# Scatters of a routed token group taken out of the routing job and spread over the attention stage

## The chip, the cores and the metric

The kernel runs on one core of one Trainium2 chip. A core has a matrix engine (TensorE; PE in the profile, its weight loads PEld), a vector engine (VectorE, DVE), an activation engine (ScalarE, ACT), a general engine (GpSimd, POOL), and a queue engine that issues most transfers (SyncE, SP). Each engine takes its instructions in the order in which they stand in its own list; between engines they wait on semaphores. The metric is the device time of one launch in microseconds (us).

## The reference

Eight sequences of 1024 tokens with 256 features go through causal attention with 16 heads, a residual, and a mixture of experts (8 experts, two chosen for each token), with a residual again.

```python
x = x + _layernorm(_L0_attn_ref(_layernorm(x), Wq, Wk, Wv, Wo))     # 16 heads of 16, causal softmax
logits = flat @ router_weight.T + router_bias                        # flat = _layernorm(x)
topk_w, topk_idx = jax.lax.top_k(softmax(logits), 2)
gu   = jnp.einsum('th,ehn->ten', flat, gate_up_proj) + gate_up_bias  # E=8, H=256, 2I=1024
glu  = min(gu[..., :I], 7) * sigmoid(1.702 * min(gu[..., :I], 7))
down = jnp.einsum('tei,eih->teh', (clip(gu[..., I:], -7, 7) + 1) * glu, down_proj) + down_bias
x = x + _layernorm((gathered(down, topk_idx) * topk_w).sum(axis=1))
```

Everything is float32. The kernel computes only the two chosen experts of a token: it sorts the tokens by expert through DRAM.

## The kernel before, in words

**Attention stage.** The work is cut into 32 units: eight sequences (b) times four groups of four heads (g). A unit has nine steps, each of them two half steps (one pair of heads each), so 18 half steps. In a half step PE computes scores for the row maxima of the unit (`sa`, line 834), the transposed scores of the unit before (`sb`, line 929) and weighted values (`av`, line 970). VectorE reduces the maxima (lines 844 to 865, 888), ScalarE takes the exponentials (line 941), and GpSimd masks the diagonal blocks (lines 883 and 950). Masks exist only in five of the nine steps; the last four steps of a unit (WHOLE) have none. A 33rd pass drains the last unit.

**Background work.** All the rest of that stage (layer norms, projections, the output projection, routing) is written as generators that yield `piece(pe, dve, act, pool, after)`: an estimated cost on four engines, and for how many half steps the next piece must wait. They are jobs in three lists: `urgent`, `due`, `back`. After each half step `pump` adds to a credit per engine and emits the pieces that are ready and that the credit allows, lists in that order, jobs in the order in which they were started. A piece's instructions stand in the engines' lists at that point; a GpSimd instruction is tied to its place by `in_order` (a scatter comes after the last ordinary GpSimd instruction before it, and the next ordinary one comes after all scatters before it).

**Groups and routing.** The 8192 tokens are 16 groups (NT) of 512; group t = 2b + c. `finish(b, c)`, a job of the list `back`, projects the attention's output (`yps`, line 1031), normalises it, adds the residual, stores it, and goes on with `route(t, ...)`: layer norm into the tile `xn2` (two buffers), transposes (`x2ps`, line 1092), router logits, the ranks of the experts on VectorE (lines 1109 to 1149), counts on PE (`cps`, line 1153), a slot per token and choice (lines 1158 to 1183), two extra columns in `xn2` (lines 1185 and 1190), and then eight indirect DMAs (two choices times four row blocks, line 1194), the scatters, which write 128 rows each to their experts' regions in DRAM. After group 12 of 16 (NT - LATE) and after the last one, `route` also builds a table (lines 304 to 439): which expert and which rows each later tile takes.

**Expert stage.** Tiles of 256 rows of one expert go through the gate and up products (`gu`, line 1470), the activation, and the down product (`dn`, line 1510). The first 16 tiles (EARLY) come from the first 12 groups alone, and go by the first table; while the first 14 of them run, `pump` is called between their products, so that the last groups are routed beside them. Ahead of tile 14 of the order, `finish_all()` emits what is left of all jobs at once, as tile 16 needs the second table. Loads run two tiles ahead. The early loads (`load_early`) stand, at the latest, after the last half step of unit 31, half step 575; if the first table is not known there, pieces are emitted one after another, with nothing between them, until it is:

```python
while NT - LATE not in known:
    emit(back, back[0])
load_early()
```

Of the kernel before, what the change touches and what calls it, by code (L numbers as in the profile page):

```python
# [24 lines left out]
def piece(pe=0.0, dve=0.0, act=0.0, pool=0.0, after=0):  # L25


    return (pe, dve, act, pool), after
# [30 lines left out]
def attn_moe_kernel(  # L59
# [15 lines left out]
    nc = tc.nc  # L75
    B, S, D = x.shape
# [4 lines left out]
    NG = H // HG  # L81
# [9 lines left out]
    NT = B * S // TB  # L91
    NTB = TB // P
    I32 = mybir.dt.int32
    TOPK = 2
    TS = 256
    TN = TS // P
# [142 lines left out]
    def in_order(put, scatter=False):  # L239

        if free[0]:
            return
        for before_it in fixed if scatter else fixed + loose:
            tc.add_manual_dep(
                put.ins, before_it,
                mybir.DependencyInfo(mybir.DependencyClass.NoSync, mybir.DependencyReason.DATA),
                reason="order of the source",
            )
        if scatter:
            loose.append(put.ins.name)  # L250
        else:
            fixed[:], loose[:] = [put.ins.name], []

    def apart(put, group):

        tc.declare_no_dep(put.ins, group=group, reason="scatters to different rows")
        tc.add_to_no_dep_group(group, put.ins)
# [30 lines left out]
    LATE = 4  # L288
# [253 lines left out]
    with ExitStack() as attn:  # L542
# [514 lines left out]
        def normed(dst, src):  # L1057
# [13 lines left out]
                )  # L1071
            yield piece(after=1)

        def route(t, x1, last):

            xn = ap2.tile([P, NTB, XD], F32, tag="xn2", name=f"xn2_{t}")
            if t >= NT - TN - 1:
                yield from normed(xn, x1)
# [109 lines left out]
            first_of = ap2.tile([P, NTB, E], F32, tag="rank", name=f"first_{t}")  # L1188
            nc.vector.tensor_tensor(first_of, is_r[:, 0], region, ALU.mult)
            nc.vector.tensor_reduce(xn[:, :, D + 1], first_of, AX.X, ALU.add)  # L1190
            for r in range(TOPK):
                for n in range(NTB):
                    yield piece(pool=1.1, after=0 if last and (n or r) else 1)
                    put = nc.gpsimd.indirect_dma_start(  # L1194
                        out=xs_dram[:, :],
                        out_offset=bass.IndirectOffsetOnAxis(ap=slots[:, t, r, n : n + 1], axis=0),
                        in_=xn[:, n, :], in_offset=None,
                    )
                    in_order(put, scatter=True)
                    apart(put, "xs")  # L1200
            if nth == NT - 1:
                yield piece(dve=0.4)
                fill_tails()
# [9 lines left out]
        def start(kind, gen):  # L1213
            job = Job(gen, now)
            kind.append(job)
            return job

        def emit(kind, job):
            job.run(now)
            if job.done:  # L1220
                kind.remove(job)
# [52 lines left out]

        early = {}

        def load_early():

            flat = x_buffer("early")
            for i in range(IN_X):  # L1280
                early[i] = flat[:, ts(i, XS)].rearrange("p (n d) -> p n d", n=TN)
                at = loaded(tables[NT - LATE][:, 1, i : i + 1], E * R)
                ahead_of(nc.sync.dma_start(out=early[i], in_=slot_rows(at)), "xs")
# [3 lines left out]
        with tc.manual_schedule(  # L1287
            engines={engines.PE, engines.DVE, engines.Activation, engines.SP}
        ):
            free[0] = False  # L1290
            jobs = {}
            wr = begin()
            more = start(due, others(wr))
            for _ in range(2 * KT):
                emit(due, more)
            jobs["v"] = start(due, values(0))
            jobs["p1"] = start(due, project(0, 1))
            second, late, whole = None, deque(), False
            for u in range(B * NG + 1):
                first = None  # L1300
                if u < B * NG:
                    b, g = divmod(u, NG)
                    if g == 1:
                        finish_by(jobs["v"], jobs["p1"])
                        if b + 1 < B:
                            jobs["x"] = start(due, prep(b + 1))
                    if g < NG - 1:
                        spread(u + 1)
                    if b + 1 < B and g == 2:
                        jobs["p0"] = start(due, project(b + 1, 0))  # L1310
                    first = maxima_tiles(u)
                for k in range(K):
                    if second:

                        for c in {t[0] for t in STEPS[k][2]}:
                            while not rows_of[u - 1, c].done:
                                emit(urgent, rows_of[u - 1, c])
                    if u == B * NG - 1 and not early and NT - LATE in known:
                        load_early()
                    if first and g == 0 and b + 1 < B and k == 5:  # L1320
                        xs[b + 1] = load_x(b + 1)
                    if first and g == NG - 1 and b + 1 < B and k == K - 2:
                        finish_by(jobs["p0"])
                        spread(u + 1)
                    if first and g == NG - 1 and b + 1 < B and k == K - 4:
                        jobs["v"] = start(due, values(b + 1))
                        jobs["p1"] = start(due, project(b + 1, 1))
                    for pair in range(2):
                        if not first and pair:
                            break  # L1330
                        heads = []
                        if first:
                            heads.append(first[0](k, pair))
                            if second:
                                heads.append(second[0](k, 1 - pair))
                        else:
                            heads += [second[0](k, 0), second[0](k, 1)]
                        for part in range(2):
                            for scores, _ in heads:
                                for hh in range(2):  # L1340
                                    scores(hh, part)


                        for _, use in reversed(heads) if first else heads:
                            use()

                        us = 1.64 + 0.62
                        of_dve = {WHOLE: 1.22, EDGE: 1.68, TWO: 0.72}[STEPS[k][0]]
                        of_act = 1.8 if STEPS[k][0] == TWO else 1.2
                        share = 0.68, us - of_dve, us - of_act, us - 0.35  # L1350
                        halves = (pair,) if first else (0, 1)
                        if first and second:
                            earn(*share)


                            if pair:
                                halves = (0, 1) if whole else (1,)
                            else:
                                whole = spend(least=1.5) is not None and bool(late) and (
                                    len({t[0] for t in STEPS[late[0][1]][2]}) == 1  # L1360
                                )
                                halves = () if whole else (0,)
                        if len(late) > DELAY - 1 or (late and not second):
                            f, kk = late[0]
                            for half in halves:
                                f(kk, half)
                            if not first or pair:
                                late.popleft()
                        if not first or pair:
                            if first:  # L1370
                                first[1](k)
                            if second:
                                second[1](k)
                                late.append((second[2], k))
                        if first and second:
                            pump(most=0.0 if whole and not pair else 1.0)
                        elif first:

                            pump(0.8, 1.2, 0.8, 1.0)
                        else:  # L1380
                            pump(1.2, 2.0, 0.8, 1.4)
                second = values_tiles(u) if first else None
                if u == B * NG - 1 and not early:
                    while NT - LATE not in known:
                        emit(back, back[0])
                    load_early()
            while late:
                f, kk = late.popleft()
                for half in range(2):
                    f(kk, half)  # L1390
            free[0] = True
# [384 lines left out]
```

## Time and profile before

| | us |
|---|---|
| median of 3 runs | 2174.46 |
| the runs | 2169.46 to 2175.39 |
| the profiled execution | 2167.24 |
| its span (first to last instruction) | 2165.1 |
| PE busy | 2057.3 (95%) |
| VectorE busy | 1708.3 (79%) |
| ScalarE busy | 1062.7 (49%) |
| GpSimd busy | 1051.7 (49%) |
| the 128 scatters (line 1194) on GpSimd | 129.1, mean 1.009 each |

Line numbers are those of the kernel before. Busy time counts a matmul from its issue to a modelled end, so a busy PE is not PE at its peak; what matters is where PE stands idle, and what it waits for. The attention stage runs to about 1348 us, its drain to 1381 us, the expert stage from there to the end. The chain of work that ended last is 71% PE, 17% VectorE and 5% GpSimd.

### The profile page before, as it was taken

How to read it: one execution, taken by the hardware profiler on the slowest of the kernel's cores; microseconds unless marked ns; L12 is line 12 of the kernel's file. 1: busy time of each engine (PE TensorE's matmuls, PEld its weight loads, DVE VectorE, ACT ScalarE, POOL GpSimd, SP SyncE). 2: the span in 40 equal slices, each digit the busy share in tenths (PEclk: the TensorE clock that was granted, in tenths of full speed). 3: DMA queues.
4: the chain of work that ended last, by engine and by line, in shares of the span. 5: the costliest groups of instructions: out<-in, count | busy, mean ns of one | idle time of the engine just before them, and what ended most of it. 6: DMA issues, size and time to landing. Idle time of an engine off the chain costs nothing.

```text
span 2165.1 us, 44591 instructions
## 1 busy us (share of the span) xinstructions
PE 2057.3 (95%) x16205; PEld 1262.3 (58%) x16205; DVE 1708.3 (79%) x4091; ACT 1062.7 (49%) x2072; POOL 1051.7 (49%) x1213
## 2 busy tenths in 40 slices
PE   7999999999999999999999998999999999999995
PEld 3444444444544434434534443678888888888884
DVE  4786886986887887887888788678778888877776
ACT  3566665666666655656655665433123232222222
POOL 3421653472474455354544645456544444444443
PEclk9999999999999999999999999999999999999998
DMA  4101102112112111112111111656867777876784
GB/s 123 23 16 44 35 26 63 32 46 46 42 32 69 24 41 46 48 36 58 46 39 41 44 39 36 207 189 208 259 242 266 269 246 262 291 241 231 268 286 150
DMA packets 147096, 254.85 MB, mean 118 GB/s; under 512 B 21504, under 2 KB 106008, under 8 KB 144952
## 3 DMA queue, kind: packets, MB, share of 16 engines
q1 hardware_dynamic: 133128, 217.01, 32.5%
q0 software_dynamic: 12528, 34.36, 4.3%
q8 instruction: 129, 2.11, 0.4%
q14 instruction: 95, 0.78, 0.1%
q10 hardware_dynamic: 1216, 0.58, 0.1%
HBM read 171.13 MB, written 55.63 MB: 105 GB/s over the span
## 4 chain that ended last, share of the span: by engine, by line
PE 71%; DVE 17%; POOL 5%; issue 3%; DMA 2%; ACT 2%; SPq 0%; DVEq 0%; ACTq 0%; POOLq 0%
PE sa L834 18%; PE gu L1470 15%; PE av L970 10%; PE dn L1510 8%; PE sb L929 6%; PE pjk L740 3%; PE yps L1031 3%; PE pjq L740 3%; PE vps L726 3%; DVE mx L850 2%; DVE sa L844 2%; DVE gate L1479 1%; PE xtps L1448 1%; DVE mx L888 1%; DVE acc L1586 1%
## 5 line engine op out<-in xcount | busy, mean ns | idle before, releaser
L941 ACT ACTIVATE pT<-sb 128x512 f32<-128x512 f32 x1134 | 616.2, 595 | 394.2 <-PE sb L929 360.6
L929 PE MATMUL sb<-qP,kP 32*128 32x512 f32 (+3 forms) x3072 | 703.6, 528 | 13.8 <-ACT pT L941 11.0
L834 PE MATMUL sa<-kP,qP 32*128 32x512 f32 (+3 forms) x3072 | 655.2, 526 | 25.5 <-DVE mx L844 12.6
L1470 PE MATMUL gu<-xsT,wg 128*128 128x256 f32 (+1 forms) x2208 | 487.5, 373 | 3.3 <-ACT xsT L1450 1.9
L1470 PEld LDWEIGHTS gu<-xsT,wg 128*128 128x128 f32 x2208 | 407.6, 191 | 59.3 <-ACT xsT L1450 4.3
L850 DVE TENSOR_REDUCE mx<-sa 128x2 f32<-128x1024 f32 x256 | 310.6, 1215 | 116.7 <-PE sb L929 96.6
L950 POOL TENSOR_SCALAR_AFFINE_SELECT pT<-pT 128x512 f32<-128x512 f32 x256 | 164.6, 659 | 468.2 <-ACT pT L941 456.1
L834 PEld LDWEIGHTS sa<-kP,qP 32*128 32x128 f32 x3072 | 226.8, 185 | 248.1 <-issue 100.0
L1481 ACT ACTIVATE sig<-gate 128x256 f32<-128x256 f32 (+1 forms) x276 | 112.8, 409 | 522.2 <-DVE gate L1479 492.0
L970 PE MATMUL av<-pT,vpad 128*32 128x256 f32 (+1 forms) x5120 | 350.0, 370 | 5.0 <-DVE avs L981 3.0
L1486 POOL TENSOR_TENSOR sig<-sig,gate 128x256 f32<-128x256 f32 (+1 forms) x276 | 195.4, 715 | 321.4 <-ACT sig L1481 317.4
L929 PEld LDWEIGHTS sb<-qP,kP 32*128 32x128 f32 x3072 | 294.9, 186 | 46.2 <-ACT pT L941 20.5
L970 PEld LDWEIGHTS av<-pT,vpad 128*32 128x32 f32 x5120 | 117.1, 109 | 292.7 <-issue 233.9
L1510 PE MATMUL dn<-wd,act 128*128 128x256 f32 x1064 | 257.7, 382 | 14.0 <-DVE act L1491 11.5
L1510 PEld LDWEIGHTS dn<-wd,act 128*128 128x128 f32 x1064 | 194.6, 190 | 45.6 <-DVE act L1491 19.4
L844 DVE CUSTOM_DVE_ANT_0 sa<-sa,cmask 128x512 f32<-128x512 f32 x256 | 177.7, 699 | 40.2 <-PE sb L929 20.8
L1479 DVE TENSOR_SCALAR gate<-gu,bs 128x256 f32<-128x256 f32 (+1 forms) x276 | 128.8, 467 | 86.2 <-PE gu L1470 70.7
L1491 DVE SCALAR_TENSOR_TENSOR act<-up,sig 128x256 f32<-128x256 f32 (+1 forms) x276 | 131.9, 478 | 49.3 <-POOL sig L1486 45.5
L1194 POOL DMA_INDIRECT xsd<-xn,slots x128 | 129.1, 1009 | 64.2 <-DVE xn L1190 34.8
L1524 POOL DMA_INDIRECT ytd<-ys,places x133 | 134.9, 1014 | 48.8 <-issue 26.9
L869 ACT COPY edge<-sa 128x512 f32<-128x512 f32 x192 | 113.0, 589 | 41.1 <-DVE mx L859 19.9
L888 DVE TENSOR_REDUCE mx<-edge 128x8 f32<-128x1024 f32 x96 | 115.7, 1205 | 17.9 <-POOL edge L883 17.9
(243 smaller groups left out, 2327.4 us busy)
## 6 DMA issues: line engine op xcount, KB each, us to landing
wg<-_L_ffn_gate_up_proj_dram SPq DMA_DIRECT2D x69, 1024.0 KB
wd<-in_L_ffn_down_proj_dram SPq DMA_DIRECT2D x69, 512.0 KB
xs<-xsd SPq DMA_DIRECT2D x60, 258.0 KB
yy<-ytd SPq DMA_DIRECT2D x15, 1024.0 KB
bs<-biasd SPq DMA_DIRECT2D x69, 132.0 KB
x<-in_L_attn_x_dram SPq DMA_DIRECT2D x16, 512.0 KB
aT<-avn SPq DMA_DIRECT2D x256, 32.0 KB
x1d<-y SPq DMA_DIRECT2D x16, 512.0 KB
```

What stands on the lines that cost most here:

```text
L834: nc.tensor.matmul(ps[:, hh, ds(at, w)], lhsT=qP[r, ts(i, P)], rhs=kP[r, ds(c * QC, w)], start=True, stop=True,)
L844: nc.vector.tensor_tensor_reduce(out=ps[:, hh, :], in0=ps[:, hh, :], in1=cmask, scale=1.0, scalar=NEG, op0=ALU.add, op1=ALU.max, accum_out ...
L850: nc.vector.tensor_reduce(mx[:, heads, i, 2:3], ps, AX.X, ALU.max)
L888: nc.vector.tensor_reduce(mx[:, :, of_two(k)[0], 1], d, AX.X, ALU.max)
L929: nc.tensor.matmul(banks[hh][:, ds(at, QC - off)], lhsT=kP[r, ts(j, P)], rhs=qP[r, ds(c * QC + off, QC - off)], start=True, stop=True,)
L941: nc.scalar.activation(pT[:, 2 * pair + hh, :], banks[hh], AF.Exp)
L950: in_order(nc.gpsimd.affine_select(out=d, in_=d, compare_op=ALU.is_ge, fill=0.0, base=0, pattern=[[0, HG], [1, P]], channel_multiplier=-1,))
L970: nc.tensor.matmul(av[ds(hh * HS, HS), ds(off + a - at, z - a)], lhsT=vp[:, j, ds((g * HG + hh) * VS, HS)], rhs=pT[:, hh, a:z],  start=c n ...
L1470: nc.tensor.matmul(ps[:, half, :w], lhsT=wg[:, kt, ds(half * FF + f * P, P)], rhs=xT[:, kt, :], start=(kt == 0), stop=(kt == KT - 1),)
L1479: nc.vector.tensor_scalar(gt, ps[:, 0, :w], bs[:, f : f + 1], LIMIT, ALU.add, ALU.min)
L1486: in_order(nc.gpsimd.tensor_tensor(sg, sg, gt, ALU.mult))
L1510: nc.tensor.matmul(pss[n][:, 0, :], lhsT=act[:, f, ts(n, P)], rhs=wd[:, f, :], start=(f == 0), stop=(f == FT - 1),)
```

## The change

The eight scatters leave `route` and become a job of their own, `scatter_rows`, in the list `back`. For groups 0 to 9 (`slow`: t < NT - LATE - TN = 10) a piece may follow the one before it only after four half steps, where it was one; for groups 10 to 14 it is one half step as before; the last group still does its own, in a row. `route(t)` now begins by waiting until group t - 2 has put all its scatters (its `xn2` buffer is the one that group t takes over). `route` itself is done, and the table is built, without waiting for the group's scatters; so the early loads ask for both: the first table known, and all scatters of groups 0 to 11 put (`early_known`). At the forced point after half step 575, the scatters that are held back are emitted first, then the first job of `back`.

```diff
+        puts = {}
+
+        def scatter_rows(t, xn, last):
+
+            slow = t < NT - LATE - TN
+            rest = 0 if last else 4 if slow else 1
+            for r in range(TOPK):
+                for n in range(NTB):
+                    yield piece(pool=1.1, after=rest if n or r else 3 if slow else 1)
+                    put = nc.gpsimd.indirect_dma_start(
...
+                    in_order(put, scatter=True)
+                    apart(put, "xs")
+
+        def scattered(t):
+            return t in puts and (t >= NT - TN or puts[t].done)
+
         def route(t, x1, last):
 
+            while t > 1 and not scattered(t - 2):
+                yield piece(after=1)
             xn = ap2.tile([P, NTB, XD], F32, tag="xn2", name=f"xn2_{t}")
...
-            for r in range(TOPK):
-                for n in range(NTB):
-                    yield piece(pool=1.1, after=0 if last and (n or r) else 1)
-                    put = nc.gpsimd.indirect_dma_start(
...
+            puts[t] = scatter_rows(t, xn, last)
+            if last:
+                yield from puts[t]
+            else:
+                puts[t] = start(back, puts[t])
...
+        def early_known():
+            return NT - LATE in known and all(scattered(t) for t in range(NT - LATE))
...
-                    if u == B * NG - 1 and not early and NT - LATE in known:
+                    if u == B * NG - 1 and not early and early_known():
                         load_early()
...
-                    while NT - LATE not in known:
-                        emit(back, back[0])
+                    while not early_known():
+                        held = [t for t in puts if t < NT - LATE and not scattered(t)]
+                        emit(back, puts[held[0]] if held else back[0])
                     load_early()
```

More of the change, by code (lines that the diff above doesn't have):

```diff
@@ L1072, in normed @@
             yield piece(after=1)
+        puts = {}
[6 more added lines that the diff above has]
+                    put = nc.gpsimd.indirect_dma_start(
+                        out=xs_dram[:, :],
+                        out_offset=bass.IndirectOffsetOnAxis(ap=slots[:, t, r, n : n + 1], axis=0),
+                        in_=xn[:, n, :], in_offset=None,
+                    )
+                    in_order(put, scatter=True)
+                    apart(put, "xs")
+        def scattered(t):
+            return t in puts and (t >= NT - TN or puts[t].done)
         def route(t, x1, last):
+            while t > 1 and not scattered(t - 2):
+                yield piece(after=1)
             xn = ap2.tile([P, NTB, XD], F32, tag="xn2", name=f"xn2_{t}")
@@ L1190, in route @@
             nc.vector.tensor_reduce(xn[:, :, D + 1], first_of, AX.X, ALU.add)
-            for r in range(TOPK):
-                for n in range(NTB):
-                    yield piece(pool=1.1, after=0 if last and (n or r) else 1)
[L1194 to L1200, printed above, removed]
+            puts[t] = scatter_rows(t, xn, last)
[3 more added lines that the diff above has]
+                puts[t] = start(back, puts[t])
             if nth == NT - 1:
```

## The prediction

> **What bounds the kernel now.** I read the page first. PE is busy for 95% of the span and 71% of the chain that ended last is PE, so time is won or lost where PE stands still. Then I cut the attention stage at the starts of its units (96 `sa` rows of line 834 each), four units, one sequence, per stretch, and added the last two units, the forced stretch after half step 575, the drain, and the end of routing in the expert stage:
>
> ```profile
> core 0: us, PE busy (x) PEld busy (x) DVE busy (x) ACT busy (x) POOL busy (x), PEclk, DMA share, GB/s
> 582.10:746.50 164.40, 161.35 (x1574) 76.19 (x1573) 136.36 (x305) 105.19 (x197) 87.95 (x96) 1.00 0.18 45
> 746.50:921.30 174.80, 167.35 (x1582) 78.00 (x1578) 140.77 (x328) 104.67 (x198) 91.04 (x99) 0.97 0.17 44
> 921.30:1095.40 174.10, 166.13 (x1582) 78.07 (x1578) 140.80 (x326) 104.47 (x198) 91.31 (x99) 0.98 0.17 45
> 1095.40:1268.60 173.20, 165.66 (x1580) 78.06 (x1576) 139.49 (x329) 103.26 (x195) 85.22 (x96) 0.98 0.16 39
> ...
> 1347.90:1353.90 6.00, 1.68 (x12) 1.28 (x10) 3.96 (x21) 0.34 (x1) 1.94 (x3) 0.67 0.01 1
> 1353.90:1381.50 27.60, 26.43 (x302) 12.09 (x301) 13.09 (x45) 18.09 (x28) 9.43 (x12) 0.89 0.52 175
> 1530.00:1560.00 30.00, 26.70 (x125) 22.77 (x124) 25.90 (x93) 4.75 (x11) 15.76 (x21) 0.94 0.91 267
> ```
>
> The same work takes 164.4 us in one sequence and 174.8, 174.1 and 173.2 in the next three, which also lose clock (0.97, 0.98). The order of time inside these three shows six places, two each, where VectorE and ScalarE both sit for 3 to 5 us as if PE were late; all six lie in or right behind four or five scatters in a row on GpSimd, in the last half steps of a unit, where no mask stands between them. One of them, GpSimd, ScalarE and VectorE:
>
> ```profile
> 775.00 0.96 POOL L1194 DMA_INDIRECT xsd<-xn,slots  x1 [0.30 <-issue]
> 776.27 0.96 POOL L1194 DMA_INDIRECT xsd<-xn,slots  x1 [0.30 <-issue]
> 777.53 0.96 POOL L1194 DMA_INDIRECT xsd<-xn,slots  x1 [0.30 <-issue]
> 778.80 0.96 POOL L1194 DMA_INDIRECT xsd<-xn,slots  x1 [0.30 <-issue]
> ```
>
> ```profile
> 774.71 1.09 ACT L941 ACTIVATE pT<-sb 128x512 f32<-128x512 f32 x2 [0.52 <-PE sb L929]
> 779.81 1.08 ACT L941 ACTIVATE pT<-sb 128x512 f32<-128x512 f32 x2 [4.01 <-PE sb L929]
> ```
>
> ```profile
> 776.48 0.18 DVE L509 BATCH_NORM_AGGREGATE mv<-st 128x2 f32<-128x6 f32 x1
> 779.70 1.23 DVE L850 TENSOR_REDUCE mx<-sa 128x2 f32<-128x1024 f32 x1 [3.04 <-PE sb L929]
> ```
>
> Scatters stand 1.27 us apart in a row; everybody resumes at 779.8, when the last ends. Last, the chain at the forced point, where routing pieces stand with nothing between them:
>
> ```profile
> 1350.97 0.18 DVE two L414
> ...
> 1351.28 0.83 PE tabps L417 x2
> ...
> 1353.22 0.14 issue
> 1353.36 0.57 PE takenps L438 x2
> 1353.93 2.02 PE sb L929 x8
> ```
>
> PE's last `av` ends at 1347.9; until 1353.9 PE has two products of the table to do and waits for VectorE between them: a forced piece costs its full latency, 6.0 us here for four pieces.
>
> **The change, part by part.** I set the order of both programs' instructions side by side. No scatter is added or dropped; places change, three in kind.
>
> *1. Fewer scatters in a row.* In the attention stage GpSimd's list had eight runs of four or five scatters: groups 0, 2, and 4 to 9. Group 2's, at 577.7 to 582.9, cost nothing visible; group 0's cost its half step 2.2 us; groups 4 to 9 are the six stalls. After the change I find one run of five (groups 4 and 5 interleaved, unit 20), two of three, the rest one or two. Three sequences at 174.8, 174.1, 173.2 against 164.4 are 28.9 us, 4.8 a stall with its lost clock. Five of six gone: -24. Bounds: -31 (all six and group 0's), 0 (the runs are not the cause).
>
> *2. The forced stretch grows.* Eight scatters at four half steps are 32 half steps, and `route(t)` waits for group t - 2, so the groups back up. In the order, group 8's scatters end in unit 31 and group 10 has only its layer norm done at half step 575, where before only the end of the table was left. Behind the last `av` now stand, one after another: three scatters of group 9, group 10's routing from its transposes on, its eight scatters, all of group 11's routing, its eight scatters, the whole table. Nothing of units 31 and 32 stands between, on PE, VectorE or ScalarE. Its latency:
> - routing from the transposes: `x2ps` 0.59, two copies 2 x 0.586, `lpsT` 0.44, copy 0.27, `lps` 0.41, VectorE lines 1109 to 1149 4.72 (the sum of the groups' means), the exponential 0.23, `cps` 0.60, VectorE lines 1158 to 1190 3.65: 12.1; eight handovers at about 0.17 (0.14 to 0.23 in the chain): 13.4;
> - eight scatters, 7 x 1.27 + 0.96 = 9.9. They are on the path: group 11's `rstd` (line 517) stands behind them on GpSimd;
> - `rstd` 1.05 and four normalisations of 1.23: 6.0;
> - group 11's routing: 13.4;
> - the table: VectorE lines 310 to 356 2.2, `segps` 0.76, copy 0.15, `firstps` 0.38, handovers 0.5, and from line 375 to the last product the measured 4.5 (1349.45 to 1353.93): 8.5. Group 11's scatters (9.9) run beside it; the drain's first masks and the early loads queue behind them, hidden while PE starts the drain and 27.6 us lie ahead of tile 0.
>
> Together 51.2, less the 6.0 of before: +45. The clock in that stretch was 0.67; at 1/0.67 the 4.1 us of products in the two routings cost 2 more. +47. Bounds: +36 (handovers nothing, and 40% of VectorE's 17 us overlapped, as neighbours at 1350.06 to 1350.34 partly are), +58 (group 11's scatters hold up the table as runs of scatters do above, twice 4.8).
>
> [...]
>
> *3. A second forced stretch.* Groups 12 to 15 start later, and at tile 14 `finish_all()`, which before found nothing left, now emits 31 pieces: group 15's routing from line 1138 on, its eight scatters, and the second table. VectorE first clears tile 13's last quarter (lines 1479 and 1483, 0.94), then 2.52, `cps` 0.6, 3.65, tails 0.35, table lines 321 to 354 4.3, `segps` 0.76, copy 0.15, `firstps` 0.38, lines 375 to 394 1.1, lines 397 to 414 2.6, `tabps` 0.83, handovers 1.0: 19.2 without PE work between. Before, these pieces lay in 1530 to 1560, where PE idled 3.3. +16. Tile 16's loads (the zeros to 1549, weights landing at 1558.4, 25 us behind the table's start) have the stretch and tiles 14 and 15 as cover; without those the wait of 25 would show. Bounds: +9 (half overlaps work queued on PE), +24 (its scatters hold VectorE up).
>
> *4. Moved work.* PE's `yps` of groups 12 and 13 (4 x 1.92) and one routing (some 2.4) go from the attention stage to the drain and the expert tiles, groups 10 and 11 into the stretch above (4.9). All of it is 15 us of PE; but units with almost none of it took 39 to 40 us (units 1 and 30) and such with much of it 39.8 to 43 (17, 16), so perhaps a third is won, 5. The drain has 1.2 us idle and the tiles 1600 to 2000 almost none, GpSimd gets 20 us more beside the early tiles, and two more activation table loads of 1.28 stand on ScalarE (idle enough): +5. Net 0; bounds -10 to +10.
>
> **Sum.** -24 + 47 + 16 + 0 = +39 on the profiled execution: 2167.2 + 39 = 2206. Its time is 7.2 under the median of the runs; carried over, 2213. I say 2211.
>
> **The rivals.**
> - *The stalls stay* (a transfer or PE itself makes them, scatters only happen to be there). For it: group 2's run of four had none. Against: six of six long waits lie there. Part 1 becomes 0: 2235.
> - *The stretches overlap more than their rows say*, both at their low bounds, 36 + 9 - 24: 2195. For it: neighbouring instructions on VectorE overlap. Against: the 6.0 us of before is what its rows add up to.
> - *Faster*: the thinned attention stage wins what the stretches cost. It would have to bring all twelve units from 746.5 to 1268.6 (43.5 each) to units 1 to 3's 38.8: 56 us, and units 4 to 17 (40.9) some 2 us each, 28: 84 against 63, 2153. It decides from a win of 70 us. Against: in 582 to 746, without stalls, PE is busy for 161 of 164 us.
> - *The change does not space the scatters.* GpSimd runs a scatter as soon as it can, whatever the plan; only masks between them hold them apart. If pairs stall too, part 1 is about halved: 2223.
>
> **How the numbers follow.** Forecast 0.62, stalls stay 0.08, overlap 0.13, spacing halved 0.11, faster 0.06. The first, the halved one and the one with the stalls are slower; so is overlap, but for low luck. A change within 0.3% (6.5 us) is about what a measurement of this kernel cannot tell from none; it would need overlap and all the low bounds: 0.03 of the 0.13, with 0.01 from the others. Faster 0.05, same 0.04, slower 0.91. The range reaches from 2185, overlap with -31 and -4 of the moved work, to 2240, the stalls staying with a little more: 0.08 is left out below, 0.08 above.
>
> **What would show it.** Right: the three sequences from unit 18 on near 164 to 168 us at clock 0.99 or more; PE idle for some 45 to 50 us in one stretch behind `av` of half step 575, with 19 scatters inside it; a second of some 17 to 20 us ahead of tile 14. Wrong: waits of 3 to 5 us on ScalarE where no scatters stand in a row; or PE working in those stretches.

## The result, and the profile after

| | us |
|---|---|
| before, median of 6 runs, the first three among them (2161.1 to 2175.4) | 2167.57 |
| after, median of 6 runs (2195.7 to 2198.3) | 2196.76 |
| ratio | 1.0129, 95% interval 1.0113 to 1.0146 |
| profiled execution, before and after | 2167.24 and 2195.73 |
| its span, before and after | 2165.1 and 2194.0 |

The changed kernel is slower by 29 us; the forecast was 2211, in a range from 2185 to 2240. A second comparison gave a larger loss, 1.0267, and much of what follows is about that difference.

The attention stage, the two stretches and the early expert tiles of the changed kernel, in windows. The columns are the window, its length, and the busy time of PE, PEld, VectorE, ScalarE and GpSimd with instruction counts, then the granted clock, the DMA share and GB/s:

```profile
576.90:741.90 165.00, 160.46 (x1576) 76.16 (x1575) 138.60 (x303) 104.91 (x198) 95.30 (x102) 1.00 0.18 46
741.90:907.50 165.60, 160.75 (x1538) 73.70 (x1538) 137.50 (x314) 102.08 (x191) 83.59 (x93) 0.98 0.19 46
907.50:1071.90 164.40, 160.50 (x1581) 76.11 (x1581) 136.87 (x305) 103.93 (x196) 82.69 (x90) 1.00 0.17 40
1071.90:1233.30 161.40, 159.57 (x1574) 75.71 (x1570) 133.81 (x300) 104.45 (x196) 69.02 (x78) 1.00 0.16 38
1303.00:1353.20 50.20, 12.22 (x70) 7.95 (x70) 21.40 (x106) 3.79 (x10) 23.71 (x24) 0.56 0.12 44
1353.20:1386.80 33.60, 31.18 (x326) 15.89 (x325) 10.96 (x33) 21.00 (x33) 12.04 (x18) 0.95 0.44 148
1386.80:1562.70 175.90, 167.06 (x848) 141.62 (x849) 133.56 (x387) 54.82 (x113) 113.56 (x126) 0.99 0.63 209
1564.70:1585.80 21.10, 4.05 (x16) 3.83 (x17) 13.81 (x66) 1.93 (x3) 10.37 (x11) 0.59 0.48 129
```

The three sequences from unit 18 on take 165.6, 164.4 and 161.4 us, where they took 174.8, 174.1 and 173.2. In 1303.0 to 1353.2 the forced pieces stand: 50.2 us with 12 us of PE, where before there were 6.0. In 1564.7 to 1585.8 the second forced stretch stands, ahead of tile 14.

The first stretch, in the order of time, PE:

```profile
1311.59 0.61 PE L1175 MATMUL cps<-chosen,ones 128*128 128x32 f32 x2
1328.43 0.47 PE L1114 MATMUL x2ps<-ident,xn 128*128 128x128 f32 x1 [16.23 <-POOL xn L529]
...
1346.41 0.98 PE L363 MATMUL segps<-ident,new 128*128 128x1 f32 x4 [5.32 <-DVE new L356]
...
1352.72 0.57 PE L438 MATMUL takenps<-each,ones 128*128 128x8 f32 x2 [1.26 <-DVE each L435]
1353.22 2.09 PE L929 MATMUL sb<-qP,kP 32*128 32x512 f32 x8
```

and what PE waited 16.23 us for, on GpSimd:

```profile
1316.17 0.95 POOL L1083 DMA_INDIRECT xsd<-xn,slots  x1 [8.51 <-issue]
...
1325.02 0.96 POOL L1083 DMA_INDIRECT xsd<-xn,slots  x1 [0.30 <-issue]
1326.01 1.04 POOL L517 TENSOR_TENSOR rstd<-ve,nhalf_seg 128x4 f32<-128x4 f32 x1
1327.15 4.83 POOL L529 TENSOR_SCALAR xn<-y,mv,rstd 128x256 f32<-128x256 f32 x4
```

Group 11's `rstd` and its four normalisations stand behind eight scatters of group 10, and its transposes behind those. The second stretch, PE:

```profile
1570.94 0.61 PE L1175 MATMUL cps<-chosen,before 128*128 128x32 f32 x2 [6.28 <-DVE chosen L1171]
...
1579.26 0.56 PE L363 MATMUL segps<-ident,new 128*128 128x1 f32 x2 [7.29 <-DVE nf L350]
...
1585.83 2.77 PE L1491 MATMUL gu<-xsT,wg 128*128 128x256 f32 x6
```

One stall is left in the attention stage, in the one run of five scatters (unit 20). GpSimd and ScalarE:

```profile
850.35 0.98 POOL L1083 DMA_INDIRECT xsd<-xn,slots  x1 [0.16 <-issue]
...
855.43 0.96 POOL L1083 DMA_INDIRECT xsd<-xn,slots  x1 [0.30 <-issue]
```

```profile
851.40 1.08 ACT L941 ACTIVATE pT<-sb 128x512 f32<-128x512 f32 x2 [0.53 <-PE sb L929]
855.95 0.60 ACT L941 ACTIVATE pT<-sb 128x512 f32<-128x512 f32 x1 [3.46 <-PE pjk L740]
```

So in this pair of profiles, in the attention stage from unit 18 on, every run of four or more scatters has its long waits (six runs before, one after). Some runs are followed, some 7 us after their last scatter, by one more wait of 3 to 4 us with no four scatters near it (834.8 and 1008.9 before, 863.6 after). It seems to follow from the stall by way of the clock, which was at 0.50 from 831.1 to 834.5 and from 1005.2 to 1008.6 before, with PE idle for 1.99 and 1.90 us ahead of that, and from 858.5 to 865.3 after, with PE idle for only 0.23 and 0.25 us. At that clock two products of `sa` took 1.22 us, at full clock 0.70.

```profile
861.38 1.22 PE L834 MATMUL sa<-kP,qP 32*128 32x512 f32 x2
```

```profile
863.61 1.09 ACT L941 ACTIVATE pT<-sb 128x512 f32<-128x512 f32 x2 [3.39 <-PE sb L929]
```

Only one such wait of before stands by itself, 3.45 us on ScalarE at 1304.8, in unit 30; on chip 10, below, it is there too (4.72 us at 1271.5).

### The profile page after: what moved, and what is told of

Read it like the earlier page. It is cut to its first block, busy times and chain, and to the rows that moved or that the text cites. A ratio compares the mean times of both kernels' runs of the same rounds, so it can differ in the third digit from the quotient of the medians.

```text
span 2194.0 us, 44614 instructions
## 1 busy us (share of the span) xinstructions
PE 2050.0 (93%) x16205; PEld 1263.8 (58%) x16205; DVE 1714.8 (78%) x4091; ACT 1065.5 (49%) x2074; POOL 1047.7 (48%) x1213
## 5 line engine op out<-in xcount | busy, mean ns | idle before, releaser
L929 PE MATMUL sb<-qP,kP 32*128 32x512 f32 (+3 forms) x3072 | 694.2, 523 | 0.5 <-issue 0.2
L950 POOL TENSOR_SCALAR_AFFINE_SELECT pT<-pT 128x512 f32<-128x512 f32 x256 | 164.2, 657 | 510.1 <-ACT pT L941 495.9
L929 PEld LDWEIGHTS sb<-qP,kP 32*128 32x128 f32 x3072 | 292.3, 184 | 29.0 <-ACT pT L941 6.9
L888 DVE TENSOR_REDUCE mx<-edge 128x8 f32<-128x1024 f32 x96 | 115.8, 1206 | 15.8 <-POOL edge L883 15.4
```

The source lines that it names most:

```text
L929: nc.tensor.matmul(banks[hh][:, ds(at, QC - off)], lhsT=kP[r, ts(j, P)], rhs=qP[r, ds(c * QC + off, QC - off)], start=True, stop=True,)
L950: in_order(nc.gpsimd.affine_select(out=d, in_=d, compare_op=ALU.is_ge, fill=0.0, base=0, pattern=[[0, HG], [1, P]], channel_multiplier=-1,))
```

## The experiments

The theory was that scatters in a row make the stalls, and that the forced pieces cost their latency. The first four runs were to tell the two prices apart. They ran on chip 11, where the kernel before took 2134.41 us (2132.1 to 2138.2), 33 us less than in the first comparison. No chip is recorded for that one.

**A limit of two scatters in a row, in the kernel before.**

```diff
                     yield piece(pool=1.1, after=0 if last and (n or r) else 1)
+                    while not free[0] and not forced and len(loose) >= 2:
+                        yield piece(pool=1.1, after=1)
...
                 if u == B * NG - 1 and not early:
+                    forced.append(True)
                     while NT - LATE not in known:
```

> The kernel before, with one rule more: a scatter of the attention stage is put off while two scatters already stand behind the last ordinary GpSimd instruction. No run of scatters is longer than two; the scatters stay in the routing job, and the forced point after half step 575 has the same four pieces as before. Runs make the stalls (my theory): the three sequences from unit 18 on fall from 174 us to 164 to 166 at a clock of 0.99 or more, nothing else moves, and the ratio to before is 0.986 to 0.989 (-24 to -31 us, six stalls at 4.8). Runs are not the cause (the thinning of the stage by work that moves out of it was what won the time): the sequences stay near 174 us, ratio 0.998 to 1.002.

Measured: 2135.8 us, ratio 1.0008 (0.9998 to 1.0018). No gain, as the rival said, but not for the rival's reason: the sequences from unit 18 on took 165.1, 164.5 and 163.6 us, not 174. The kernel before was that fast there too.

**The limit, and groups 10 and 11 held back to the forced point.**

```diff
+            while t in (10, 11) and not forced:
+                yield piece(after=1)
             xn = ap2.tile([P, NTB, XD], F32, tag="xn2", name=f"xn2_{t}")
```

> The limit of two scatters in a row, and in addition the routing of groups 10 and 11 waits for the forced point after half step 575: 79 forced pieces there against 4 (70 in the changed kernel), and 39 pieces ahead of tile 14 against none (31 in the changed kernel). The scatters of groups 0 to 9 are as in the run with the limit alone. If the forced stretches cost what the profile of the changed kernel shows (44 and 21 us) and the work moved into them and behind them is worth about 16 to 20 us to the attention stage: 50 to 65 us over the run with the limit alone, so ratio to before 1.01 to 1.02. If the price of the changed kernel comes from the waits of its spread scatters and not from the forced pieces: no more than 10 us over the run with the limit, ratio 0.99.

Measured: 2206.7 us, ratio 1.0338 (1.0321 to 1.0355), 71 us over the limit alone. Its two stretches, in windows:

```profile
1296.90:1357.40 60.50, 14.30 (x70) 8.83 (x70) 23.44 (x115) 3.70 (x9) 25.87 (x25) 0.53 0.08 30
1574.80:1596.30 21.50, 4.99 (x34) 4.31 (x35) 14.49 (x69) 2.08 (x4) 15.11 (x16) 0.57 0.57 167
```

This kernel keeps its scatters in the routing job, so pieces late enough to be forced make the loss by themselves; spread scatters are not needed for it. By the profiles, against the limit alone: attention stage -19, first stretch +55, drain +6, early tiles +8, second stretch +23, sum +71 as measured. The stage won as much as expected (16 to 20); the expectation of 50 to 65 was short by a first stretch of 60.5 us for its 79 pieces and by the drain and the tiles.

**A job of its own, without the four half steps.**

```diff
-            slow = t < NT - LATE - TN
+            slow = False
```

> The changed kernel without the four half steps: scatters are a job of their own, one each half step for all groups. Runs of four and five stand in the order as before, the forced point has no more pieces than before, and 17 pieces (two scatters and the second table) are forced ahead of tile 14. My theory: the six stalls stay (sequences of 173 to 175 us from unit 18 on), no stretch at 1303 to 1353, and some 8 to 12 us of stretch ahead of tile 14: ratio 1.003 to 1.007. Rival (the job of its own already spreads or wins something): below 0.997.

Measured: 2142.3 us, ratio 1.0034 (1.0022 to 1.0047), inside the expectation; but no stalls, though its runs of four and five scatters stood in GpSimd's order of time as before. The second stretch, here 17 pieces, most of them the second table's, costs 15.8 us against a profile of before on the same chip (33.1 and 17.3 between the same two `gu` rows), and tile 0 starts 5.4 us earlier. The stretch:

```profile
1517.40:1531.90 14.50, 3.13 (x14) 2.95 (x14) 10.32 (x41) 0.42 (x1) 8.52 (x9) 0.60 0.68 193
```

**Eight scatters in a row, in the kernel before.**

```diff
-                    yield piece(pool=1.1, after=0 if last and (n or r) else 1)
+                    yield piece(pool=1.1, after=0 if n or r else 1)
```

> The kernel before, with the scatters of each group emitted without a half step between them: three runs of eight and one of six stand in the order where before there were eight runs of four or five; the other groups have runs of three or fewer between masks. If a stall lasts from about the third scatter to the end of the run (7 us for a run of eight, and 1 to 2 us of lost clock): 3 x 8.5 + 5 is 30 us against 31 before, ratio 0.998 to 1.002. If a stall has a fixed length (4.8 us a run): 4 runs at 4.8 are 19, ratio 0.993 to 0.996. If it is scatters in a row at any length, ratio over 1.005.

Measured: 2140.3 us, ratio 1.0017 (1.0005 to 1.0030). The number is that of the first expectation, its premise is not: no sequence from unit 18 on has more than 165.2 us, and in its three runs of eight PE is never idle. Here eight in a row do PE no harm. The small loss is not theirs alone: this profile is 4.1 us behind that of before on the same chip already at the third unit (101.6 against 97.5 us), ahead of any scatter.

So the stalls were missing on this chip. The next question was whether they belong to the kernel at all. Both kernels and the limit ran again, unchanged, on chip 10:

> The kernel before, unchanged, for a profile beside the next two. In the runs so far it took 2161 to 2175 us in one place and 2132 to 2138 in another. If the stalls depend on the chip and not on the program: where it takes some 2134 us, its sequences from unit 18 on are 163 to 165 us with runs of four and five scatters in them, and GpSimd's scatters have the same times and distances (0.96 and 1.27 us) as where it took 2167. If the 33 us lie elsewhere (transfers of the expert stage, the clock): the sequences are 173 to 175 us as in the profile before.

> The changed kernel, unchanged. Where before has no stalls (2134 us), it has nothing to win but thinner units, and pays both stretches: +44 and +21 and 8, less 16 to 20 of work moved out of the attention stage: 2185 to 2197, ratio 1.022 to 1.030. Where before has them (2167 us), 1.011 to 1.015 as measured first.

> The limit of two scatters in a row again, beside a profile of before. Where before has no stalls: ratio 0.999 to 1.002. Where before takes 2161 us or more: its three sequences from unit 18 on fall to 164 to 166 us, ratio 0.984 to 0.989. If the limit doesn't matter even there, 0.998 to 1.002.

Measured there: before 2135.1 us, the changed kernel 2193.7, ratio 1.0267 (1.0250 to 1.0284), and the limit 1.0000 (0.9990 to 1.0010). All three as expected for a before without stalls. The kernel before on chip 10, the three sequences from unit 18 on:

```profile
742.70:906.90 164.20, 160.57 (x1582) 76.31 (x1578) 140.89 (x328) 104.73 (x198) 91.50 (x99) 1.00 0.18 47
906.90:1071.20 164.30, 160.38 (x1584) 76.61 (x1581) 140.58 (x326) 104.53 (x197) 91.63 (x99) 1.00 0.18 47
1071.20:1235.00 163.80, 159.85 (x1578) 76.38 (x1574) 139.32 (x329) 103.37 (x195) 85.66 (x96) 1.00 0.17 41
```

It is the same program as in the first comparison, with the same instruction counts to within three, the same busy times on VectorE, ScalarE and GpSimd to within 0.5 us, and it takes 9.4 to 10.6 us less in each. The run of five scatters that made the stall shown in the prediction, GpSimd and ScalarE on chip 10:

```profile
769.92 0.98 POOL L1194 DMA_INDIRECT xsd<-xn,slots  x1 [0.16 <-issue]
771.20 0.96 POOL L1194 DMA_INDIRECT xsd<-xn,slots  x1 [0.30 <-issue]
...
775.00 0.96 POOL L1194 DMA_INDIRECT xsd<-xn,slots  x1 [0.30 <-issue]
```

```profile
770.91 1.08 ACT L941 ACTIVATE pT<-sb 128x512 f32<-128x512 f32 x2 [0.53 <-PE sb L929]
773.04 1.09 ACT L941 ACTIVATE pT<-sb 128x512 f32<-128x512 f32 x2 [1.05 <-PE sb L929]
```

Same scatters, same 0.96 us, same 1.27 us apart, and ScalarE goes on after 1.05 us where it waited 4.01. The changed kernel on chip 10:

```profile
743.00:903.70 160.70, 156.87 (x1538) 72.80 (x1538) 137.44 (x314) 101.92 (x191) 83.78 (x93) 0.99 0.19 47
903.70:1068.70 165.00, 161.06 (x1582) 76.13 (x1582) 137.46 (x308) 104.61 (x197) 83.39 (x91) 1.00 0.17 40
1068.70:1230.90 162.20, 159.51 (x1574) 75.45 (x1570) 133.84 (x296) 103.87 (x195) 68.70 (x78) 0.99 0.16 37
1300.20:1350.40 50.20, 12.27 (x72) 8.01 (x73) 21.43 (x106) 3.81 (x10) 23.83 (x24) 0.56 0.12 44
1562.00:1583.20 21.20, 4.08 (x17) 3.84 (x17) 13.84 (x66) 1.93 (x3) 10.39 (x11) 0.59 0.48 134
```

Both stretches are as long as in the first profile, to 0.1 us; its last stall, in unit 20, is gone (40.4 us for the unit against 46.0).

**Once more before and the limit; and three half steps.** On chip 11 again, and the limit a last time on chip 7, in search of a place where before stalls:

> The kernel before, unchanged, once more for its profile. If it takes 2160 us or more, the six stalls should stand at the scatters in a row again (sequences of 173 to 175 us from unit 18 on); if about 2135 us, none (162 to 165 us).

> The limit of two scatters in a row, a third time. Beside a before of 2160 us or more: 0.984 to 0.989, if runs of scatters are what the stalls need; 0.998 to 1.002 if they are not. Beside a before of some 2135 us: 0.999 to 1.001, as twice before.

> The limit of two scatters in a row, a last time, in case the kernel before takes over 2160 us beside it as it did in the first comparison. Then: 0.984 to 0.989, if the stalls need four or more scatters in a row; 0.998 to 1.002, if they do not. Beside a before of some 2135 us: 0.999 to 1.001, and the question stays open.

Measured: before 2133.3 us in the profiled run, its three sequences 164.2, 164.3 and 163.8; the limit 0.9999 (0.9990 to 1.0009) on chip 11 and 1.0001 (0.9991 to 1.0011) on chip 7, where before took 2135.5. The stalls did not come back on any of three chips (on chip 7 before is known by its time alone; the profile of the limit there has none), so whether the limit would cure them could not be tried.

Then the changed kernel with three half steps in place of four between the scatters of a slow group, and one in place of three ahead of its first:

```diff
-            rest = 0 if last else 4 if slow else 1
+            rest = 0 if last else 3 if slow else 1
...
-                    yield piece(pool=1.1, after=rest if n or r else 3 if slow else 1)
+                    yield piece(pool=1.1, after=rest if n or r else 1)
```

> The changed kernel with three half steps between scatters in place of four: 21 forced pieces after half step 575 (against 70, and none with one half step), 17 ahead of tile 14 (against 31; 17 also with one half step). If a forced piece costs about what it cost in the changed kernel (50 us for 70, 60 for 79, 6 for 4: 0.7 to 0.8 us a piece), the first stretch is 13 to 18 us, the second 13 to 15, and the ratio is 1.007 to 1.011. If the backlog has a price of its own beside the pieces (later groups, thinner and thicker units): over 1.014.

Measured: 2157.6 us, ratio 1.0107 (1.0091 to 1.0122), at the upper end of the expectation. Its stretches:

```profile
1304.80:1320.10 15.30, 3.90 (x20) 3.38 (x17) 10.26 (x55) 0.57 (x2) 6.75 (x7) 0.58 0.15 52
1532.30:1546.80 14.50, 3.12 (x14) 2.95 (x14) 10.32 (x41) 0.42 (x1) 8.52 (x9) 0.62 0.68 192
```

The first stretch grows with what is forced: 5.6 to 6.0 us for 4 pieces, 15.3 for 21, 50.2 for 70, 60.5 for 79. The second is 14.5 for 17 pieces, with one half step as with three, 21.2 for 31, and 21.5 for 39.

**Nothing forced.** One half step for all groups, groups 12 to 15 with their scatters in the routing again, and some VectorE credit in the early expert tiles, so that the last groups are done in time:

```diff
-            slow = t < NT - LATE - TN
+            slow = False
...
-            return t in puts and (t >= NT - TN or puts[t].done)
+            return t in puts and (t >= NT - LATE or puts[t].done)
...
-            if last:
+            if t >= NT - LATE:
                 yield from puts[t]
...
-                pump(0.6, 0.0, 0.6, 0.35)
+                pump(0.6, 0.30, 0.6, 0.35)
...
-            pump(0.6, 0.0, 0.6, 0.35)
+            pump(0.6, 0.30, 0.6, 0.35)
```

> The changed kernel with one half step between scatters for all groups, groups 12 to 15 putting their scatters themselves as before, and 0.30 us of VectorE credit per call in the early expert tiles where there was none: nothing is forced, at either place. If the forced pieces are the whole loss: no stretch at either place, the 5.6 us of before gone as well, ratio 0.995 to 0.998 beside a before of 2135 us. If pieces on VectorE beside the expert tiles hold its products up: 1.000 to 1.004.

Measured: 2136.8 us, ratio 1.0012 (1.0003 to 1.0021): the second expectation. No stretch is left, and the first product of tile 0 comes 7.1 us earlier than in before on the same chip (1340.7 against 1347.8). But the early tiles up to tile 13 take 11.4 us more, this kernel and before:

```profile
1340.70:1525.20 184.50, 167.06 (x824) 140.98 (x825) 139.71 (x444) 53.89 (x110) 106.11 (x118) 0.97 0.63 202
```

```profile
1347.80:1520.90 173.10, 166.43 (x828) 141.18 (x829) 133.40 (x414) 53.71 (x110) 102.92 (x115) 0.98 0.64 209
```

There are 30 VectorE instructions more in that window, 6.3 us busy, and 3.2 us more of GpSimd, PE's work is the same to 0.6 us, and it is 11 us longer. So work put beside the early tiles is not free either; which of the two engines held them up is not shown. No version was found that beats the kernel before.

## Why the prediction was right, step by step

Both pairs of profiles, cut at the same places: the last `av` of the attention stage, the first `sb` after it, the first `gu`, the 441st `gu` row (in tile 13), the 496th (behind the second stretch), and the end. After less before, in us, rounded after the difference was taken:

| | forecast | first pair | chip 10 |
|---|---|---|---|
| attention stage | -24 (part 1) and -5 (part 4) | 1303.0 - 1347.9 = -44.9 | 1300.2 - 1315.4 = -15.2 |
| first stretch | +47 | 50.3 - 5.9 = +44.3 | 50.2 - 5.6 = +44.6 |
| drain and tiles up to 13 | +5 (part 4) | 3.8 + 4.2 = +8.0 | 4.2 + 3.7 = +7.8 |
| second stretch | +16 | 38.7 - 17.4 = +21.4 | 38.7 - 20.0 = +18.7 |
| the rest | 0 | +0.1 | +2.1 |
| sum | +39 | +28.9 | +58.0 |

**Part 2, the forced stretch: right, in size and in its parts.** Group 10's routing took 12.5 us from 1302.9 (forecast 13.4), the scatters 9.8 from 1316.2 (9.9), `rstd` and the normalisations 6.0 (6.0), group 11's routing 12.3 from 1332.0 (13.4), the table 9.0 (8.5). Group 11's scatters ran beside the table and held nothing up; the high bound of +58 had counted on that. PE was busy for 12.2 us of the 50.2, so it was idle for 38.0, not for 45 to 50 as the sign in the prediction said; the length of the stretch, which the chain of waits sets, was as forecast. Of the clock: it was 1.00 until 1309 and 0.50 from there to the end of the stretch. The 16 products of `lpsT` took 0.92 us at 1304.90 and 1.40 at 1333.30, a row of two `cps` products 0.61 in both routings (1311 and 1340), against 0.38 to 0.41 in the attention stage at full clock: half as much again at a clock of 0.50. The 2 us that the forecast added for the clock do not show: both routings were shorter than the 13.4 without it. In the first profile of before the clock fell to 0.50 behind each of the six stalls too, for 3.4 to 6.8 us, and PE had stood idle for no more than 1.9 to 2.1 us in a row there.

**Part 3, the second stretch: right in place and kind, too small by 3 to 5 us.** The stretch itself was 21.1 us for 19.2. The rest is about the credit of 3.3 us that I took for idle time in 1530 to 1560: it does not show, as the tiles up to 13 took 4 us more, not less, with those pieces gone from them. These rows do not separate it from the moved work of part 4.

**Part 4, moved work: wrong in size.** "Perhaps a third is won, 5": chip 10, where no stall hides it, shows that the whole 15 us of PE work taken out came off the attention stage, 15.2. What was given back in the drain and the tiles was 8, not 5. Net -7 (-5 with the rest counted), inside the bounds of ±10.

**Part 1, the stalls: right for that place, and not a property of the kernel.** In the first pair the stage gained 44.9, of which 15.2 are thinner units, if these are worth the same there as on chip 10; the other 29.7, by difference, are stalls, against -24. Measured by place, the six units that stalled in the first profile of before took 29.7 us more there than on chip 10, where I had put 28.9, and group 0's run cost its unit 2.2; the changed kernel kept one stall, 5.6 us in unit 20, in the run of five that the prediction had named. The reading "everybody resumes when the last ends" holds for the stall that the prediction shows and not for all: in units 19, 23 and 27 ScalarE went on 1.3 to 1.4 us after the last scatter had ended. My bounds of -31 and 0 held. But what I took for a cost of four or five scatters in a row needs something more, which the first place had and three chips did not. There the term is zero, and the kernel loses 58 us, not 29. The forecast for a case without gain from stalls, 2235, stood at +63 on the profile before and had a chance of 0.08, for the reason "a transfer or PE itself makes them". As an account of the difference it was the nearer one on chip 10.

**The sum.** +28.9 was measured where +39 was forecast: the stalls gave 5.7 and the moved work 7 more than forecast and the first stretch cost 3 less, while the second cost 5 more and offset a part of that. The rest of the distance from 2211 to 2197 is the level of before, which I had put at 2172 and which six runs put at 2168. And that part 1 came out at all was luck with the place: the forecast took one profile's stalls for the kernel's own.

**The rivals.** That the stretches overlap more than their rows say fell: they were 50 and 21 us. That pairs stall fell: the changed kernel has 16 pairs ahead of 1300 us in its first profile, and none stalled. That a thinner stage wins was the right mechanism at 15 us and far from the 70 that it needed.

What stays open is the cause of the stalls. Shown is that in the first pair of profiles they stand at runs of four or more scatters, and that such runs do not suffice. Transfers do not tell the places apart: in the 7 us around the run shown in the prediction, 369 packets and 0.81 MB were moved, and 374 and 0.81 MB around the same run on chip 10. In the first profile of before, PE's rows around the stall:

```profile
776.10 0.59 PE L834 MATMUL sa<-kP,qP 32*128 32x512 f32 x2
...
777.22 0.69 PE L929 MATMUL sb<-qP,kP 32*128 32x512 f32 x1
777.74 0.59 PE L834 MATMUL sa<-kP,qP 32*128 32x512 f32 x2
777.75 0.59 PE L929 MATMUL sb<-qP,kP 32*128 32x512 f32 x1
780.46 1.22 PE L929 MATMUL sb<-qP,kP 32*128 32x512 f32 x1 [2.12 <-ACT pT L941]
```

VectorE's reduction of 779.70 waited for the products of 776.10, which by these rows (their ends are modelled) ended at 776.69. On chip 10 the same products ran at 772.30, and VectorE began 0.05 us after they ended:

```profile
772.30 0.59 PE L834 MATMUL sa<-kP,qP 32*128 32x512 f32 x2
```

```profile
772.94 1.23 DVE L850 TENSOR_REDUCE mx<-sa 128x2 f32<-128x1024 f32 x1
```

So it looks as if PE was not slow, but word of its results came 3 us late; PE itself went on with its next products at 777.2 and stood still only at 778.3, when it needed ScalarE. The rows of `sb` with x1 are not lost products: the others of their pairs ran from 780.46 on, and this profile has all 3072 products of `sb`, as that of chip 10 has.

What is lost are records of semaphores. The trace of before holds 26854 of their updates and that of the changed kernel 27704, in the first pair; the same two programs have 29965 and 30042 on chip 10, and no other profile has fewer than 29921. Up to the first scatter, at 351 us, nothing is missing (4730 against 4725). In the 8 us from the start of the seven runs of scatters with a stall (groups 0 and 4 to 9) there are 49 to 78, against 181 to 225 at the same runs on chip 10; at group 2's run, which had none, 66 against 115; at the one stalled run of the changed kernel 60 against 157. They go on missing in the expert stage, 7360 against 8106 from the 496th `gu` row to the end, and that part takes 592.5 us in the one place and 592.2 in the other: there the loss of records alone cost no time. It shows in the list of transfers too: in the first pair alone it has no time from issue to landing for the scatters. Before, and the same list on chip 10, where they land after 2.8 us:

```profile
xsd<-xn,slots POOLq DMA_INDIRECT x128
```

```profile
xsd<-xn,slots POOLq DMA_INDIRECT x128, 2.8
```

So the stalls come with a loss of such records, from the first scatters on, and only in the first place. Whether what loses the records also holds up the updates themselves, whether recording them makes the stalls, or whether both follow from something else there, no run shows, and as the stalls did not come back, it could not be tried. And where records are missing, the name of the engine that ended a wait ("<-PE sb L929") is uncertain, as it is inferred from them.

## What to carry to other kernels

Work that is forced at a point where nothing stands beside it costs its whole latency, and that can be added up from rows of the profile before: here the sum of handovers, scatters, normalisations and table was 51.2 us, 53 with the clock, and the stretch took 50.2. A planner's spacing rule is to be followed through to its last deadline, as a wait of four half steps, harmless in each place, moved two groups' routing behind the last attention work. And a stall seen in one profile is a fact of that run: before a gain is booked on its removal, the same program is profiled in another place, and the two profiles are compared in what they record, not only in what they time.

## What was not expected of the hardware

- The same program took 2161 to 2175 us in the first runs and 2131 to 2139 on chips 7, 10 and 11. Against chip 10 the difference lies in the attention stage (1347.9 against 1315.4 us; all that follows it took 817.2 against 819.7), and there 29.7 of the 32.5 us lie in the six units with stalls at scatters in a row.
- The two profiles with stalls lack 8 to 10% of the semaphore updates that the same programs have on chip 10, and in the 8 us from the start of a stalled run some two thirds of them.
- Eight scatters in a row, 10 us of GpSimd, left PE busy throughout in the attention stage on chip 11.
- In the early expert tiles 6.3 us more of VectorE work (and 3.2 us more of GpSimd) went with 11.4 us more time, although VectorE was busy for only 77% of the window before (133.4 of 173.1).
